# Layer 3 of a four-layer residual network: four of nine depthwise taps moved from TensorE to VectorE, instance-norm scaling moved to ScalarE

**Chip, cores, metric.** One Trainium2 chip, one of its cores. The time is device time in microseconds (us) from the first to the last instruction; lower is better. Unless a spread is given, times are medians of four executions of one kernel in one session (seven for the kernel before, where it was run beside others). The record calls a run slow when it is over 1.5% above the fastest of its kernel; the profiled execution of the kernel before had a mean granted TensorE clock of 0.969 of full speed.

## What is computed

Input x is 4 images of 256 channels and 48 x 48 pixels, f32. Four residual layers follow each other, each on a group norm of x. Layers 0 to 2 are attention, a gate and a second attention, take 4000 us of the 4355 and are not touched. The change is in layer 3:

```python
# x = x + layer3(_gn(x)); in layer3, with x the normalised input:
p = jnp.mean(x, axis=(2, 3))
h = jax.nn.leaky_relu(p @ attn_w1.T, 0.01)
a = jax.nn.sigmoid(h @ attn_w2.T)
y = x * a[:, :, None, None]
y = conv_general_dilated(y, refine_w, padding='SAME', feature_group_count=C)  # 3x3 depthwise
y = y + refine_b[None, :, None, None]
mu = jnp.mean(y, axis=(2, 3), keepdims=True)
var = jnp.mean(jnp.square(y - mu), axis=(2, 3), keepdims=True)
y = (y - mu) * jax.lax.rsqrt(var + 1e-5)
return jax.nn.leaky_relu(y, 0.01)
```

## The kernel before

Channels are split into two halves (k = 0, 1) of 128 partitions; an image half is a tile of 128 x 2304 in SBUF, the on-chip memory. The depthwise convolution runs on TensorE: each tap is a product with a diagonal 128 x 128 matrix, on shifted windows of a padded tile, summed in PSUM, the memory that holds TensorE's sums until another engine reads ("evicts") them. What prepares image b + 1 is a generator (`fill`) that is advanced between the chunks of image b, so that its small steps lie among the work of image b.

```python
def rsqrt(o, i):                              # L157, on GpSimd
    nc.gpsimd.tensor_tensor(o, i, mhalf[:, : i.shape[1]], ALU.pow)

def before_conv(b):                           # prepares image b
    for k in range(NK):
        for s in range(NSL):
            ps = w_mul(b, k, s)               # a matmul that finishes layer 2 (L663)
            nc.scalar.activation(tmp, ps[:, :SL], AF.Identity, bias=..., scale=...)
            nc.gpsimd.tensor_add(X[b][:, k, cols], X[b][:, k, cols], tmp)
            yield
    yield from gn(b, norm)   # 12 bn_stats, aggregate gn_mv, matmul L174, gn_gm, gn_dev,
                             # gn_sq, matmul L184, gn_gv, gn_rs (GpSimd), gn_nb
    ...                      # pm, small matmul, hl, small matmul, sigmoid
    nc.vector.tensor_mul(rsa, norm["rs"], ga)
    nc.vector.tensor_mul(nba, norm["nb"], ga)
    for k in range(NK):
        nc.scalar.activation(pad_of(b, k)[:, 1 : 1 + HW, 1 : 1 + HW], X[b][:, k, :]...,
            AF.Identity, bias=nba[:, k : k + 1], scale=rsa[:, k : k + 1])
    yield

def conv(b, k):
    for c in range(NSL // 2):                 # three chunks of 768 pixels
        ps = sc_tile()
        for h in range(2):
            for t in range(9):
                nc.tensor.matmul(ps[:, h, :SL]..., lhsT=diag[:, k, t, :],
                    rhs=pad[:, r0 + dr : r0 + dr + RS, dc : dc + HW],
                    start=t == 0, stop=t == 8)
        nc.scalar.activation(z[:, cols]..., ps[:, :, :SL], AF.Identity, bias=...)
        for h in range(2):
            nc.vector.bn_stats(st[:, 2 * c + h, :], z[...])
        yield
    nc.vector.bn_aggr(mv, st...)
    nc.vector.tensor_scalar(ve, mv[:, 1:2], IN_EPS, None, ALU.add)
    rsqrt(ri, ve)
    nc.vector.tensor_scalar(z, z, mv[:, 0:1], ri, ALU.subtract, ALU.mult)
    nc.vector.scalar_tensor_tensor(z, z, SLOPE, z, ALU.mult, ALU.max)
    nc.gpsimd.tensor_add(X[b][:, k, :], X[b][:, k, :], z)
    nc.sync.dma_start(ov[:, k, b, :], X[b][:, k, :])
```

## Time and profile before

| | before |
|---|---|
| time, 3 executions before the prediction | 4355.51 us (4351.93 to 4355.94) |
| layer 3: first tap to the end | 4005.5 to 4354.3 us |
| from the first tap of an image to that of the next | 86.2, 86.1, 85.8 us |
| last image, first tap to the end | 90.6 us |
| TensorE records of taps | 864, 293 us |

The names of lines differ between kernels, because the lines move: taps on TensorE L870 before, L873 after; eviction into z L877 and L880; scaling L891 (VectorE) and L902 (ScalarE); leaky step L892 and L903; the last addition on GpSimd L893 and L904; its short additions L819 and L822; padding L851 and L854. The taps on VectorE are L888, new.

### The profile page before, as it was taken

What the parts mean: (1) busy time and instruction counts of PE and PEld (TensorE: products, weight loads), DVE (VectorE), ACT (ScalarE), POOL (GpSimd) and SP (SyncE); (2) the same over time, 40 slices, a digit from 0 to 9 for tenths busy, and PEclk for the clock granted to TensorE, in tenths of its full rate; (3) what the DMA queues carried; (4) which work ended last, traced back from release to release, by engine and by line L of the source; (5) the groups of instructions that cost most, each with busy time, mean ns of one, the idle gap of its engine ahead of it and who ended that gap; (6) DMA issues with size and microseconds to landing.
All of it is one profiled execution on the core that took longest, in us unless ns stands there. A gap on an engine that the chain in (4) does not pass through costs nothing.

```text
span 4354.3 us, 50890 instructions
## 1 busy us (share of the span) xinstructions
PE 4078.9 (94%) x19922; PEld 1805.3 (41%) x19922; DVE 2952.5 (68%) x3719; ACT 1857.8 (43%) x3054; POOL 1065.0 (24%) x632
## 2 busy tenths in 40 slices
PE   7999999999989999999899999998899978899997
PEld 4444444444433344444333444443334433444554
DVE  4555556556989865579898655798975699754222
ACT  3444444444444444444444444444444323343211
POOL 1222222222222322222323222223232221223231
PEclk9999999999999999999999999999999988997999
DMA  4000000000000000000000000000000000000000
GB/s 146 15 15 19 12 15 8 19 15 15 12 11 12 15 12 19 12 15 12 11 15 12 12 19 15 12 15 8 8 1 1 1 1 1 1 1 1 22 33 34
DMA packets 44330, 67.50 MB, mean 16 GB/s; under 512 B 4336, under 2 KB 42032, under 8 KB 42032
## 3 DMA queue, kind: packets, MB, share of 16 engines
q1 hardware_dynamic: 41216, 62.92, 4.7%
q8 instruction: 158, 2.59, 0.3%
q10 hardware_dynamic: 2864, 1.24, 0.1%
q14 instruction: 92, 0.75, 0.1%
HBM read 54.71 MB, written 9.44 MB: 15 GB/s over the span
## 4 chain that ended last, share of the span: by engine, by line
PE 68%; DVE 27%; issue 2%; ACT 2%; POOL 1%; DMA 0%; DVEq 0%; ACTq 0%; POOLq 0%
PE sc L223 24%; PE av L242 23%; DVE acc L262 7%; DVE l1acc L564 7%; PE sc L870 7%; PE pj L397 5%; PE pj L441 3%; PE pj L409 2%; DVE acc L255 2%; DVE rinv L272 2%; PE pj L267 1%; PE pj L663 1%; ACT pt L229 1%; DVE xs L374 1%; PE pj L641 1%
## 5 line engine op out<-in xcount | busy, mean ns | idle before, releaser
L229 ACT ACTIVATE pt<-sc 128x768 f32<-128x768 f32 x1944 | 1473.7, 808 | 1524.1 <-PE sc L223 1429.3
L259 POOL TENSOR_TENSOR half<-pt 128x768 f32<-128x768 f32 x432 | 852.7, 1974 | 2630.6 <-ACT pt L229 2317.2
L223 PE MATMUL sc<-q,k 64*128 64x384 f32 x6912 | 1364.9, 513 | 52.2 <-ACT pt L229 49.4
L242 PE MATMUL av<-pt,v 128*64 128x384 f32 x6912 | 1322.7, 503 | 0.0
L262 DVE TENSOR_TENSOR acc<-acc,pt 128x768 f32<-128x768 f32 x864 | 947.8, 1097 | 128.0 <-ACT pt L229 42.2
L223 PEld LDWEIGHTS sc<-q,k 64*128 64x128 f32 x6912 | 596.5, 187 | 811.3 <-ACT pt L229 304.9
L242 PEld LDWEIGHTS av<-pt,v 128*64 128x64 f32 x6912 | 433.5, 137 | 726.2 <-issue 714.4
L255 DVE TENSOR_TENSOR acc<-acc,half 128x768 f32<-128x768 f32 x432 | 416.4, 964 | 192.0 <-POOL half L259 191.2
L564 DVE SCALAR_TENSOR_TENSOR l1acc<-pd,grid,l1acc 128x256 f32<-128x256 f32 x640 | 347.2, 542 | 18.2
L272 DVE RECIPROCAL rinv<-pj 128x384 f32<-128x384 f32 x108 | 275.9, 2555 | 110.7 <-PE pj L267 110.6
L397 PE MATMUL pj<-xs,w 128*128 128x384 f32 x768 | 303.1, 520 | 40.2 <-issue 32.7
L870 PE MATMUL sc<-pad,diag 128*128 128x384 f32 x864 | 293.0, 499 | 4.5 <-ACT pad L851 4.5
L402 ACT ACTIVATE pj<-pj 128x384 f32<-128x384 f32 x192 | 91.2, 475 | 402.6 <-DVE q L401 266.1
L870 PEld LDWEIGHTS sc<-pad,diag 128*128 128x128 f32 x864 | 165.8, 194 | 130.0 <-issue 16.0
L397 PEld LDWEIGHTS pj<-xs,w 128*128 128x128 f32 x768 | 136.2, 193 | 186.0 <-issue 101.5
L441 PE MATMUL pj<-o,wo 128*128 128x384 f32 x384 | 175.8, 540 | 39.2 <-DVE x L450 16.5
L450 DVE TENSOR_TENSOR x<-pj,x 128x384 f32<-128x384 f32 x144 | 79.9, 555 | 170.1 <-PE pj L441 170.1
L223 PE MATMUL sc<-qv,kd 64*128 64x384 f32 x864 | 176.6, 527 | 19.1 <-ACT pt L229 19.1
L242 PE MATMUL av<-pt,qv 128*64 128x384 f32 x864 | 192.1, 534 | 0.0
L409 PE MATMUL pj<-w,xs 128*128 128x128 f32 x1152 | 152.8, 283 | 13.7 <-DVE x L450 12.2
L409 PEld LDWEIGHTS pj<-w,xs 128*128 128x128 f32 x1152 | 139.2, 193 | 60.2 <-issue 28.9
L252 DVE TENSOR_TENSOR acc<-pt 128x768 f32<-128x768 f32 x108 | 107.1, 992 | 45.4 <-ACT pt L229 45.1
(137 smaller groups left out, 2102.4 us busy)
## 6 DMA issues: line engine op xcount, KB each, us to landing
xs<-in_x_dram SPq DMA_DIRECT2D x96, 384.0 KB, 3.3
x<-in_x_dram SPq DMA_DIRECT2D x8, 1152.0 KB, 8.6
out_dram<-x SPq DMA_DIRECT2D x8, 1152.0 KB, 4.2
w<-in_wqkv_dram SPq DMA_DIRECT2D x32, 192.0 KB, 3.7
wo<-in_wout_dram ACTq DMA_DIRECT2D x1, 512.0 KB, 4.8
dw<-in_dww_dram ACTq DMA_DIRECT2D x1, 132.0 KB, 5.4
wph<-in_thphi_w_dram ACTq DMA_DIRECT2D x2, 64.0 KB, 4.6
Ww<-in_W_w_dram ACTq DMA_DIRECT2D x2, 64.0 KB, 5.3
```

What stands on the lines that cost most here:

```text
L223: nc.tensor.matmul(ps[:, h, :SL], lhsT=u["of"]["k"][r, j * P : (j + 1) * P], rhs=u["of"]["q"][r, u["qc"]], start=True, stop=True,)
L229: nc.scalar.activation(pt, ps[:, :, :SL], AF.Exp)
L242: nc.tensor.matmul(u["av"][r, :SL], lhsT=value(u, j, h), rhs=pt[:, h, :], start=j == 0, stop=j == JB - 1,)
L255: nc.vector.tensor_add(u["acc"], u["acc"], u["half"])
L259: nc.gpsimd.tensor_add(u["half"], pts[0], pts[1])
L262: nc.vector.tensor_add(u["acc"], u["acc"], pt)
L272: nc.vector.reciprocal(u["rinv"], u["l"][:, :SL])
L397: nc.tensor.matmul(ps[:, :SL], lhsT=w[:, k, t, :], rhs=xs[s][:, k, :], start=k == 0, stop=k == NK - 1,)
L409: nc.tensor.matmul(ps[:, i * P : (i + 1) * P], lhsT=xs[s][:, k, i * P : (i + 1) * P], rhs=w[:, k, 2, :], start=k == 0, stop=k == NK - 1,)
L441: nc.tensor.matmul(ps[:, :SL], lhsT=wo[:, p, k * P : (k + 1) * P], rhs=o, start=True, stop=True)
L564: nc.vector.scalar_tensor_tensor(acc, src, w, acc, ALU.mult, ALU.add)
L870: nc.tensor.matmul(ps[:, h, :SL].rearrange("p (r c) -> p r c", c=HW), lhsT=diag[:, k, t, :], rhs=pad[:, r0 + dr : r0 + dr + RS, dc : dc + HW],
```

## The change

The intent: TensorE is full in layer 3, so four taps of nine go to VectorE as a fused multiply-add over the whole half, and one pass over z goes from VectorE to ScalarE to make room. The statistics move behind the taps, since they need the finished sum.

```diff
-    diag = lp.tile([P, NK, 9, P], F32, name="diag")
+    PE_TAPS = (0, 1, 2, 3, 5)
+    DVE_TAPS = (4, 6, 7, 8)
+    diag = lp.tile([P, NK, len(PE_TAPS), P], F32, name="diag")
 ...                                   (building the diagonals: the same, for PE_TAPS only)
-                for t in range(9):
+                for t in PE_TAPS:
 ...
-            for h in range(2):
-                s = 2 * c + h
-                nc.vector.bn_stats(st[:, s, :], z[:, s * SL : (s + 1) * SL])
             yield
+        zr = z.rearrange("p (r c) -> p r c", c=HW)
+        for t in DVE_TAPS:
+            dr, dc = divmod(t, 3)
+            nc.vector.scalar_tensor_tensor(
+                zr, pad[:, dr : dr + HW, dc : dc + HW], rfw[:, k, t : t + 1], zr,
+                ALU.mult, ALU.add,
+            )
+        for s in range(NSL):
+            nc.vector.bn_stats(st[:, s, :], z[:, s * SL : (s + 1) * SL])
 ...
-        nc.vector.tensor_scalar(z, z, mv[:, 0:1], ri, ALU.subtract, ALU.mult)
+        nc.vector.scalar_tensor_tensor(mr, mv[:, 0:1], -1.0, ri, ALU.mult, ALU.mult)
+        nc.scalar.activation(z, z, AF.Identity, bias=mr, scale=ri)
```

More of the change, by code (lines that the diff above doesn't have):

```diff
@@ L789, in usual_path @@
     nc.vector.tensor_add(bi2, bi2, vec[:, V_B2, :])
-    diag = lp.tile([P, NK, 9, P], F32, name="diag")
+    PE_TAPS = (0, 1, 2, 3, 5)
+    DVE_TAPS = (4, 6, 7, 8)
+    diag = lp.tile([P, NK, len(PE_TAPS), P], F32, name="diag")
     for k in range(NK):
-        for t in range(9):
-            nc.gpsimd.tensor_scalar(diag[:, k, t, :], ident, rfw[:, k, t : t + 1], None, ALU.mult)
+        for i, t in enumerate(PE_TAPS):
+            nc.gpsimd.tensor_scalar(diag[:, k, i, :], ident, rfw[:, k, t : t + 1], None, ALU.mult)
     W2 = HW + 2
@@ L867, in conv @@
                 r0 = (2 * c + h) * RS
-                for t in range(9):
+                for t in PE_TAPS:
                     dr, dc = divmod(t, 3)
@@ L871, in conv @@
                         ps[:, h, :SL].rearrange("p (r c) -> p r c", c=HW),
-                        lhsT=diag[:, k, t, :],
+                        lhsT=diag[:, k, PE_TAPS.index(t), :],
                         rhs=pad[:, r0 + dr : r0 + dr + RS, dc : dc + HW],
-                        start=t == 0, stop=t == 8,
+                        start=t == PE_TAPS[0], stop=t == PE_TAPS[-1],
                     )
@@ L890, in conv @@
         rsqrt(ri, ve)
-        nc.vector.tensor_scalar(z, z, mv[:, 0:1], ri, ALU.subtract, ALU.mult)
+        mr = small.tile([P, 1], F32, tag="in_mr", name="in_mr")
+        nc.vector.scalar_tensor_tensor(mr, mv[:, 0:1], -1.0, ri, ALU.mult, ALU.mult)
+        nc.scalar.activation(z, z, AF.Identity, bias=mr, scale=ri)
         nc.vector.scalar_tensor_tensor(z, z, SLOPE, z, ALU.mult, ALU.max)
```

## The prediction

- A "lock" is here no more than a name for what the traces show: a VectorE and a GpSimd instruction that run together, and one or both last longer by up to the time of the other. The kernel before shows it for pairs of additions like the one quoted (3.44 us for 2.02 and 2.59 for 1.80). That a tap and an addition do the same, and that the one that starts later waits until the other ends, was an estimate in the prediction; the changed kernel then showed it (a tap of 6.40 us for 2.62, begun 1.06 us after an addition of 5.03 us and done 2.43 us after it).
- 2.62 us for a tap: in the kernel before, passes of VectorE with two operands take 958 ns for 768 columns (L262) and 2558 for the 2304 of L892. On the line through both, 256 columns take 425 ns; the layer 1 taps take 485, 0.06 us more, and 2.56 + 0.06 is 2.62. This is an estimate from those three medians.
- "Cold", and the 1.7 us charged for it: in the kernel before the granted clock was 0.87, 0.89 and 0.79 in the first chunk of the first three images and 1.00 in the second. That a stall of 3 us would bring such a dip too, the one us taken off the sum, is my estimate and was not shown.

> **What bounds the kernel now.** I read the page first, then the last stage alone. The change touches only layer 3, so the first question is where layer 3 lies and what sets its length. The groups by line, for the last 455 us:
>
> ```profile
> L870 PE MATMUL sc<-pad,diag 128*128 128x384 f32 x864 | 293.0, 499 | 4.5 <-ACT pad L851 4.5
> ...
> L893 POOL TENSOR_TENSOR x<-x,z 128x2304 f32<-128x2304 f32 x8 | 40.4, 5051 | 26.6 <-DVE z L892 26.6
> ...
> L892 DVE SCALAR_TENSOR_TENSOR z<-z 128x2304 f32<-128x2304 f32 x8 | 21.4, 2674 | 0.1
> ...
> L891 DVE TENSOR_SCALAR z<-z,in_mv,in_ri 128x2304 f32<-128x2304 f32 x8 | 13.8, 1728 | 5.7 <-POOL in_ri L157 5.7
> ```
>
> The reader is to see that the nine diagonal taps (L870, two records for each f32 matmul) are busy for 293 us, start at 4005.5 us and wait for almost nothing, while the other engines have little. The waits say the same from the other side:
>
> ```profile
> ACT z L877 <- PE sc L870: 257.7, 24, 12.3
> ```
>
> The chain that ended last shows two things besides: what lies between the convolution of one image and that of the next, and what follows the last one. First the border between image 0 and 1, then the end:
>
> ```profile
> 4072.99 11.72 PE sc L870 x36
> ...
> 4084.86 0.17 DVE gn_gv L186
> ...
> 4085.10 0.71 POOL gn_rs L157
> ...
> 4086.12 0.41 PE pj L828 x4
> ...
> 4089.37 2.21 ACT pad L851
> ...
> 4091.72 8.48 PE sc L870 x21
> ```
>
> ```profile
> 4263.66 72.47 PE sc L870 x216
> 4336.15 0.91 ACT z L877
> 4337.08 1.03 DVE in_st L883 x2
> 4339.37 1.49 DVE z L891
> 4340.89 2.57 DVE z L892
> 4343.62 5.00 POOL x L893
> ```
>
> So TensorE binds except for a border of 7 us per image (convolution ends at 4084.7, the next begins at 4091.7) and a tail of 12.5 us plus 5.7 us of the last store. One chunk (768 pixels, 18 matmuls, 36 records) takes 11.65 us, an image 86.1 us from first matmul to first matmul (4005.5, 4091.7, 4177.9, 4263.7).
>
> [...] In the timeline of layer 1, the same pair of adds takes 2.02 us alone and 3.44 us beside a GpSimd add, which itself grows to 2.59 us from its usual 1.80:
>
> ```profile
> 1172.18 3.44 DVE L262 TENSOR_TENSOR acc<-acc,pt 128x768 f32<-128x768 f32 x2
> 1180.40 2.02 DVE L262 TENSOR_TENSOR acc<-acc,pt 128x768 f32<-128x768 f32 x2
> 1172.22 2.59 POOL L259 TENSOR_TENSOR half<-pt 128x768 f32<-128x768 f32 x1 [9.60 <-DVE acc L255]
> ```
>
> [...] L892, a two-input operation of that size, has a median of 2558. [...] the pad writes (L851) take 2305 ns. [...] the first chunk after each border took 13.3 to 14.6 us against 11.65, so I charge about 1.7 us.
>
> **Removed from TensorE.** 4 of 9 taps: 384 of 864 records. A chunk becomes 20/36 of 11.65 = 6.45 us, an image saves 6 x 5.2 = 31.2 us, all four 125 us (2.9%). This would be the gain if nothing else changed.
>
> **Added to VectorE.** 32 taps over 2304 elements, both inputs in SBUF, each waiting for the one before (in place). L892 is the same operation with an immediate, 2.55 us. The layer 1 taps have a pointer scalar and a strided window like the new ones:
>
> ```profile
> L564 DVE SCALAR_TENSOR_TENSOR l1acc<-pd,grid,l1acc x640: 461/485/2131, 1145.2 to 3710.2; 128x256 f32<-128x256 f32 x160
> ```
>
> [...] a tap is 2.62 us, 2.65 with the gap: 85 us in all. L891 leaves VectorE (13.8 us) and becomes ScalarE work of about 2.3 us each. By sums VectorE has per image some 8 x 2.65 + 12 x 0.5 (stats) + 12 x 0.5 (group-norm stats) + 2 x 2.6 + 2 = 40 us, and TensorE 39 + 9 (the twelve L663 products at 0.74) = 48 us. TensorE would still be the longer, so the question is the order. GpSimd builds 10 diagonals instead of 18 (5 us less), but its next operation on the path (L157, at 3977.4) waits for VectorE; no gain.
>
> **The order.** The listing of both programs shows that VectorE now runs the group norm of image b+1 in between the taps of image b: statistics 9 to 12 between the four taps of half 0, and gn_nb, hl, hl, rsa/nba each behind one tap of half 1. The pad of the next image, which TensorE needs, thus waits for all four taps of half 1, whose input is the last chunk. On GpSimd gn_rs stands behind the 5.05 us addition of half 0's result. I walk through one image, t = 0 at its first matmul:
>
> - TensorE: chunk 0 to 8.1 (cold), chunks 1 and 2 and five products to 24.7; ScalarE evacuates, z of half 0 is whole at 25.7.
> - Four taps of half 0. After each a statistic waits for a GpSimd addition (0.99 us), which the tap just locked out, and the next tap is then locked out by the next addition: about 3.65 us a tap. They end at 40.3. Six statistics (0.47 each) to 43.6, the group-norm aggregate at 43.9.
> - TensorE: chunks 0 and 1 of half 1 and four products end near 41.1; then the small matmul L174 wants that aggregate: a stall of about 3 us, new. Rest of chunk 2 until E = 50.2.
> - ScalarE scaling 45.8 to 48.1, leaky step (L892's successor) to 50.7. GpSimd starts its 5.05 us addition at 50.85, just before tap 1 of half 1 gets its input (51.2): tap 1 is locked out until 55.9 and ends at 58.5. Then gn_rs to 59.2, gn_nb, pm; tap 2 to 62.2; hl; tap 3 to 65.05; hl, sigmoid; tap 4 to 67.9; rsa, nba; pad 68.3 to 70.5. Next image at 70.6.
>
> The border grows from 7 to about 20 us and an image shrinks only from 86.1 to 70.6: 15.5 us saved of 31.2, three times, 46.5.
>
> **The last image** has no filling. Chunks end at 40.5. Half 0: taps 22 to 32.7, scaling, leaky step to 42. Half 1: tap 1 to 44.6, GpSimd's addition of half 0 takes the lock to 49.7, taps 2 to 4 to 57.6, statistics 60.5, aggregate and reciprocal root 62.1, ScalarE 64.4, leaky 67, addition 72.2, store 78. Before: 90.6 us. Saved 12.5: of 31.2, some 18.7 go to the longer tail.
>
> **Sum.** 46.5 + 12.5 = 59; one us off for a dip of the clock after the new stall: 58. Time 4355.5 - 58 = 4298 us, -1.3%.
>
> **Rivals.**
> 1. Full gain: VectorE's 40 us hide beside 48 us of TensorE, only a border of about 9 us and the tail of four taps (10.5 us) remain: about 4250 us. For it: the sums, and 150.6 us that VectorE waits for ScalarE now. Against: the order puts the pad behind the taps.
> 2. The same order, but the lock costs little (GpSimd fits between, or TensorE's stall at L174 vanishes): a border of 15 us, 3 x 23 + 18 = 87 saved, 4268 us. For it: only an overlap of a few tenths decides who gets the lock. Against: even unlocked, gn_rs stays behind the 5 us addition on its queue.
> 3. VectorE becomes the bound: taps of 4 us and more by locks, image 80 us: 4325 us. For it: layer 1 taps reach 2131 ns. Against: GpSimd has only about 22 us of additions per image.
> 4. Slower: would need over 31 us lost per image. I see nothing that large.
>
> **Range and chances.** My walk uses measured durations; its uncertain part is who wins the lock, some 2 to 5 us per image, and the clock after longer borders, 1 to 2. That makes 15 us each way common. Range 4275 to 4325. Over 2% faster (below 4268) needs rival 1 or the lucky end of 2: 0.09. Slower by 2%: 0.01.
>
> **What would show it.** Right: 480 records of taps; about 6.45 us a chunk; image starts 70 us apart; L174 waiting some 3 us for the aggregate; pads waiting for nba behind tap 4, border 18 to 21 us; mean tap above 3 us, minimum near 2.6; last matmul to end about 37 us instead of 18. Wrong: image starts 63 us or less apart (rivals 1, 2), a mean tap near 2.6, the pad ready before the last taps, or a border below 15 us.

## More of the kernel before

The view that the prediction leaves out is the load of each engine in one stretch. Its columns are: the stretch in us, its length, then the busy time (and the number of instructions) of TensorE, TensorE's weight loads, VectorE, ScalarE and GpSimd, the granted clock, the DMA share and GB/s. First the three images from first tap to first tap, in the kernel before:

```profile
4005.49:4263.66 258.17, 249.07 (x750) 139.22 (x751) 69.61 (x133) 52.30 (x63) 69.68 (x49) 0.96 0.06 23
```

TensorE works 249 of 258 us, VectorE 70. That is the invitation for the change: one engine is full, three are three quarters empty.

## The result, and the profile after

The changed kernel takes 4289.84 us (4288.64 to 4290.33), the kernel before 4354.71 us in the same session (4351.93 to 4355.94). The ratio is 0.9852, with a 95% interval of 0.9834 to 0.9869: 1.5% faster, inside the predicted range of 4275 to 4325 us. (Ratios here are the mean time of one kernel's fast runs over that of the other's fast runs of the same rounds, so not quite the ratio of the medians quoted.)

| | before | predicted | after |
|---|---|---|---|
| time | 4355.5 | 4298 | 4289.8 us |
| first tap of layer 3 | 4005.5 | | 4002.4 us |
| image periods | 86.2, 86.1, 85.8 | 70.6 | 69.2, 68.7, 69.7 us |
| last image | 90.6 | 78 | 77.9 us |
| border: L184, which follows the last tap, to the next image's first tap | 7.2 | 20 | 19.3 us |

In the two profiled executions the saving is 66.5 us: 50.7 in three periods, 12.7 in the last image and 3.1 before layer 3. Up to there the programs differ only in the diagonals that GpSimd builds (10 for 18, 5.8 us for 10.5), and TensorE was already 3.1 us ahead when that began (its L663 products just before start at 3955.6 us for 3958.7). I do not count these 3.1 as an effect: executions of the kernel before differ by 4 us among themselves.

The same view of load as above, for the three periods of the changed kernel:

```profile
4002.35:4209.87 207.52, 159.38 (x463) 86.69 (x463) 130.71 (x154) 63.62 (x68) 93.73 (x48) 0.86 0.07 29
```

No engine is full now: TensorE works 159 of 208 us, VectorE 131. TensorE saved 90 us of work, and only 51 of them came through. So the end must be set by an order of waits. (The granted clock fell from 0.96 to 0.86 in these views, but that is not where the time went: the first chunk of the first three images took 1.4 to 3.0 us longer than the second in the changed kernel, 8.15 to 9.67 for 6.72 us, at a granted clock of 0.65 to 0.83 for 1.00, and 1.4 to 2.8 us before, 13.32 to 14.63 for 11.88, at 0.79 to 0.89 for 1.00.) The groups by line of the changed kernel over its last 390 us (busy us, mean ns of one, then the idle time of the engine before them):

```profile
L873 PE MATMUL sc<-pad,diag 128*128 128x384 f32 x480 | 169.1, 510 | 5.7 <-ACT pad L854 5.7
L888 DVE SCALAR_TENSOR_TENSOR z<-pad,rfw,z 128x2304 f32<-128x2304 f32 x32 | 102.1, 3190 | 30.8 <-ACT z L880 30.6
...
L822 POOL TENSOR_TENSOR x<-x,tmp 128x384 f32<-128x384 f32 x48 | 69.8, 1471 | 74.6 <-ACT tmp L818 74.6
...
L904 POOL TENSOR_TENSOR x<-x,z 128x2304 f32<-128x2304 f32 x8 | 42.7, 5332 | 31.6 <-DVE z L903 31.6
```

The taps on TensorE are 480 records and 169 us, as counted. A tap on VectorE takes 3.19 us in the mean, though the view of that one line gives its shortest, median and longest as 2610, 2619 and 7271 ns: most are short, a few wait inside. The border between image 0 and 1 in the timeline (start, duration, engine, line, what it does, idle time before it) shows where:

```profile
4052.32 5.03 POOL L904 TENSOR_TENSOR x<-x,z 128x2304 f32<-128x2304 f32 x1 [5.27 <-DVE z L903]
...
4053.38 6.40 DVE L888 SCALAR_TENSOR_TENSOR z<-pad,rfw,z 128x2304 f32<-128x2304 f32 x1 [0.66 <-ACT z L880]
4057.31 3.02 POOL L157 TENSOR_TENSOR gn_rs<-gn_gv,mhalf 128x2 f32<-128x2 f32 x1
...
4060.51 2.61 DVE L888 SCALAR_TENSOR_TENSOR z<-pad,rfw,z 128x2304 f32<-128x2304 f32 x1
...
4065.81 2.62 DVE L888 SCALAR_TENSOR_TENSOR z<-pad,rfw,z 128x2304 f32<-128x2304 f32 x1
...
4068.42 0.15 DVE L852 TENSOR_TENSOR nba<-gn_nb,ga 128x2 f32<-128x2 f32 x1
...
4069.06 4.51 ACT L854 ACTIVATE pad<-x,nba,rsa 128x2304 f32<-128x2304 f32 x2
...
4071.51 3.96 PE L873 MATMUL sc<-pad,diag 128*128 128x384 f32 x7 [0.56 <-ACT pad L854]
```

The taps of image 0 on TensorE ended at 4052.2. The first VectorE tap of half 1 starts while GpSimd's addition runs, and is not done until 2.4 us after it. gn_rs, an operation on two columns, starts after the addition and finishes only 0.55 us after that tap. Then every small step of image 1 waits for one tap; nba is last, and TensorE starts image 1 at 4071.5. The end of the chain that ended last has the same pair in the last image, a tap of 7.28 us:

```profile
4252.60 2.54 DVE z L888
4255.16 7.28 DVE z L888
4262.46 2.63 DVE z L888
4265.12 2.63 DVE z L888
4267.77 2.87 DVE in_st L893 x6
...
4277.13 5.03 POOL x L904
```

### The profile page after: what moved, and what is told of

Its sections match the earlier page's. It is cut to its first block, busy times and chain, and to the rows that moved or that the text cites. A ratio compares the mean times of both kernels' runs of the same rounds, so it can differ in the third digit from the quotient of the medians.

```text
span 4287.8 us, 50150 instructions
## 1 busy us (share of the span) xinstructions
PE 3954.9 (92%) x19538; PEld 1733.6 (40%) x19538; DVE 3034.9 (71%) x3751; ACT 1875.7 (44%) x3062; POOL 1088.3 (25%) x624
## 4 chain that ended last, share of the span: by engine, by line
PE 64%; DVE 29%; issue 3%; ACT 2%; POOL 2%; DMA 0%; DVEq 0%; ACTq 0%; POOLq 0%
PE sc L223 24%; PE av L242 23%; DVE acc L262 8%; DVE l1acc L564 7%; PE pj L397 5%; PE pj L441 3%; PE pj L409 2%; DVE acc L255 2%; PE sc L873 2%; DVE rinv L272 2%; DVE z L888 2%; PE pj L267 1%; PE pj L663 1%; ACT pt L229 1%; DVE xs L374 1%
## 5 line engine op out<-in xcount | busy, mean ns | idle before, releaser
L259 POOL TENSOR_TENSOR half<-pt 128x768 f32<-128x768 f32 x432 | 853.8, 1976 | 2626.5 <-ACT pt L229 2313.1
L262 DVE TENSOR_TENSOR acc<-acc,pt 128x768 f32<-128x768 f32 x864 | 946.1, 1095 | 128.1 <-ACT pt L229 42.3
L873 PE MATMUL sc<-pad,diag 128*128 128x384 f32 x480 | 169.1, 510 | 5.7 <-ACT pad L854 5.7
L252 DVE TENSOR_TENSOR acc<-pt 128x768 f32<-128x768 f32 x108 | 107.1, 992 | 45.2 <-ACT pt L229 44.8
L166 DVE BATCH_NORM_STATS2 gn_st<-x 128x6 f32<-128x384 f32 x192 | 98.1, 549 | 57.4 <-POOL x L822 57.4
```

What stands on the lines that cost most here:

```text
L259: nc.gpsimd.tensor_add(u["half"], pts[0], pts[1])
L262: nc.vector.tensor_add(u["acc"], u["acc"], pt)
L873: nc.tensor.matmul(ps[:, h, :SL].rearrange("p (r c) -> p r c", c=HW), lhsT=diag[:, k, PE_TAPS.index(t), :], rhs=pad[:, r0 + dr : r0 + dr + ...
```

## The experiments

Theory: TensorE's saving is genuine (125 us), but about half of it is lost, because (a) the four long taps of a half stand in VectorE's queue before small operations that the next image needs, (b) GpSimd's operations and VectorE's taps lock each other out, (c) in the last image the taps stand behind TensorE. Rivals: VectorE is simply full; or the scaling on ScalarE is what helped or hurt. Twelve kernels were run, in four sessions, each on another chip by the record. In these the kernel before took 4352.2 to 4353.9 us; the changed kernel was not run again, its 4289.84 us belong to the session in which the kernel before took 4354.7. So the medians may be compared to about 3 us. In four expectations a phrase is cut at the mark: three gave the rival a reason that no run here shows; the fourth, of the scaling alone, named a rate of the pass that was not measured (that rival was: taking the scaling off VectorE relieves the border by itself).

### No taps on VectorE at all

```diff
-        for t in DVE_TAPS:
-            ... nc.vector.scalar_tensor_tensor(zr, pad[...], rfw[:, k, t : t + 1], zr, ...)
```

Wrong on purpose: the output lacks four taps (relative error 0.25).

> The changed kernel with the four VectorE taps simply left out (wrong result on purpose): what TensorE's saving is worth when nothing is put on VectorE. My theory (125 us less of taps on TensorE, of which the taps on VectorE give back about 60 at the image borders and in the tail): about 4232 us, image starts 55 us apart. Rival (the taps hide, and the lost gain is due to something else, such as the clock after shorter bursts or the scaling on ScalarE): close to the changed kernel, 4280 us or more.

Measured 4228.09 us (4225.18 to 4232.65), ratio 0.9714, at a mean granted clock of 0.970 for 0.963 with the taps. The saving of TensorE's part is 125 us, as counted from the records, and VectorE's taps cost 61.7 us of it, though they are busy for only 102 us of the 285 that layer 3 lasts with them. By the profiles the loss is 44.8 us in the three periods (162.7 us without these taps, 207.5 with them) and 17.4 us in the last image (60.6 and 77.9). Of the 44.8, 39.5 are the three borders together (17.7 and 57.2 us) and 4.7 three new stalls at L174.

### The scaling alone

```diff
+    PE_TAPS = tuple(range(9))
+    DVE_TAPS = ()
 ...                          (bn_stats again inside the chunk loop, as in the kernel before)
```

> Nine taps on TensorE and statistics per chunk as before, only the scaling on ScalarE. My theory: it is off the path but for the last image, where 2.3 us on ScalarE and one small operation stand for 1.5 us on VectorE: 4355 to 4358 us, same within 0.1%. Rival [...]: 4345 us or less.

Measured 4354.61 us (4353.95 to 4357.13), ratio 1.0005 with an interval of 0.9989 to 1.0022. The scaling on ScalarE (2.30 us a pass for 1.73 on VectorE) is worth nothing by itself; gain and loss come with the taps. What the scaling is worth beside taps on VectorE was not tested.

### The long taps of half 1 behind the next image's small steps

```diff
+        last["nba", b] = nc.vector.tensor_mul(nba, norm["nb"], ga)
 ...
+            tap = nc.vector.scalar_tensor_tensor(
 ...
+            if k == 1 and t == DVE_TAPS[0] and b + 1 < B:
+                after_(tap, last["nba", b + 1])     # order on VectorE, no semaphore
```

> The changed kernel with one order edge per image: tap 1 of half 1 comes behind the last group-norm operation of the next image (nba) on VectorE. Theory (the pad waits because four taps stand before it): the border shrinks from 19.4 to about 12 us, as gn_rs still waits for the 5 us addition on GpSimd; 3 times 7 us: about 4269 us. Rival (VectorE's amount of work is the bound, not its order): no gain, 4285 to 4295.

Measured 4268.89 us (4268.17 to 4271.94), ratio 0.9808. Periods of 61.0, 62.1 and 62.5 us for 69.2, 68.7 and 69.7: part (a) of the theory is worth 21 us. What is left of the border in this kernel (11.1 us) is mainly one wait (TensorE is idle for 5.8 us before the next small product), in its timeline:

```profile
4052.97 5.03 POOL L915 TENSOR_TENSOR x<-x,z 128x2304 f32<-128x2304 f32 x1 [5.27 <-DVE z L914]
...
4057.96 0.70 POOL L157 TENSOR_TENSOR gn_rs<-gn_gv,mhalf 128x2 f32<-128x2 f32 x1
4058.69 0.16 DVE L190 SCALAR_TENSOR_TENSOR gn_nb<-gn_gm,gn_rs 128x2 f32<-128x2 f32 x1 [5.34 <-POOL gn_rs L157]
```

gn_rs (now at its usual 0.70 us, as no tap runs) stands in GpSimd's queue behind the 5 us addition. The next experiment takes it out of there.

### In addition, GpSimd's addition behind gn_rs

```diff
+        add = nc.gpsimd.tensor_add(X[b][:, k, :], X[b][:, k, :], z)
+        if k == 0 and b + 1 < B:
+            held.append((add, b + 1))               # later: after_(add, gn_rs of b + 1)
```

> As e3_hold, and the addition of half 0 on GpSimd comes behind gn_rs of the next image. Theory: the border falls to the 7 us of before; 3 times 12 us against the changed kernel: about 4254 us. Rival (the addition on GpSimd costs nothing): same as e3_hold.

Measured 4268.62 us (4267.08 to 4271.73), no change: the expectation failed by 15 us. The order did change as meant, and the timeline of this kernel shows what took its place:

```profile
4055.63 0.69 POOL L157 TENSOR_TENSOR gn_rs<-gn_gv,mhalf 128x2 f32<-128x2 f32 x1 [5.74 <-DVE gn_gv L186]
4056.29 5.03 POOL L918 TENSOR_TENSOR x<-x,z 128x2304 f32<-128x2304 f32 x1
4056.36 4.98 DVE L190 SCALAR_TENSOR_TENSOR gn_nb<-gn_gm,gn_rs 128x2 f32<-128x2 f32 x1 [0.81 <-POOL gn_rs L157]
```

gn_rs is done early, GpSimd goes straight on to its addition, and gn_nb, a VectorE operation on two columns with both operands in SBUF, comes 0.07 us later and lasts 4.98 us in place of 0.16. One 5 us wait was exchanged for another.

### GpSimd's last addition replaced by fills

```diff
-        nc.gpsimd.tensor_add(X[b][:, k, :], X[b][:, k, :], z)
-        nc.sync.dma_start(ov[:, k, b, :], X[b][:, k, :])
+        nc.gpsimd.memset(z, 0.0)
+        last["fill", b, k] = nc.gpsimd.memset(z, 0.0)
+        nc.sync.dma_start(ov[:, k, b, :], z)
 ...                                   (and gn_rs of b + 1 kept behind the fills of half 0)
```

> Wrong on purpose: GpSimd's last addition x + z (two operands read from SBUF, 5.03 to 5.3 us) is replaced by two fills of z with zeros, which only write SBUF and take about as long together; the transfer out sends z, and the small gn_rs keeps its place behind the fills. Order and volume of everything else stay. Theory (the long VectorE taps are held up by GpSimd's addition, and not merely late): the tap that took 6.40 us at the border and the one that took 7.28 us in the last image fall to 2.6 us each, gn_rs falls from 3.02 to 0.7 us. At each of the three borders some 2.3 to 3 us go, in the last image some 4.6 us: about 4276 us in all, between 4273 and 4280. Rival (those taps are long for another reason, for example they wait for the activation's write or for the profiler's modelled ends): nothing moves, 4286 to 4290.

Measured 4274.62 us (4274.3 to 4276.17), ratio 0.9818. Its output is wrong (relative error 1.0). The kernel is otherwise the changed one, taps in their old place. The view of the taps' line (shortest, median, longest in ns) and the border's first steps:

```profile
L899 DVE SCALAR_TENSOR_TENSOR z<-pad,rfw,z x32: 2611/2619/2882, 4029.2 to 4250.2; 128x2304 f32<-128x2304 f32 x32
```

```profile
4052.22 2.02 POOL L915 MEMSET z<- 128x2304 f32 x1 [5.19 <-DVE z L914]
...
4053.35 2.62 DVE L899 SCALAR_TENSOR_TENSOR z<-pad,rfw,z 128x2304 f32<-128x2304 f32 x1 [0.66 <-ACT z L891]
4054.30 2.02 POOL L916 MEMSET z<- 128x2304 f32 x1
4056.28 0.69 POOL L157 TENSOR_TENSOR gn_rs<-gn_gv,mhalf 128x2 f32<-128x2 f32 x1
```

No tap is longer than 2.88 us, gn_rs is back at 0.69, and the tap runs undisturbed beside the fills, which only write. So the 6.4 and 7.3 us were made by GpSimd's reading addition. The kernel is 15.2 us faster than the change; the two fills took 4.06 us for the addition's 5.03, and gn_rs stands behind them, so about 1 us at each of three borders, and 1 us after the last leaky step, is the shorter work. Part (b), for this one operation, is worth 11 to 15 us.

### The taps by chunk

```diff
+            for t in DVE_TAPS:                      # inside the chunk loop, on 768 pixels
+                nc.vector.scalar_tensor_tensor(zr, pad[:, 2*c*RS + dr : 2*(c+1)*RS + dr, ...], ...)
+            for h in range(2):
+                nc.vector.bn_stats(...)
             yield
```

> The four taps and bn_stats work on one chunk of 768 pixels right after its eviction, in place of one pass over the 2304 pixels of a half after its three chunks. VectorE then does 96 taps of 768 elements for 32 of 2304; by the 2.62 us of the long form and the fixed part that the short ones show, a tap takes about 1.02 us, so VectorE works some 14 us longer in all. Theory (what is left of the change is lost because a half's taps come in one block behind its last chunk, where gn_st, gn_nb and the last statistics have to queue behind them): the wait at L174 of 2.9 us and the long border go, border about 12 us for 19.4, and the last image ends some 13 us sooner since only one chunk's taps stand behind TensorE's last chunk. Sum 3 times 8 to 9 and 13: about 4250 us, between 4245 and 4260. Rival (VectorE's work is the bound, its place does not matter): slower than the change by up to the 14 us, 4288 to 4304.

Measured 4270.75 us (4268.25 to 4272.68), ratio 0.981: 19 us faster than the change, but 21 short of the expectation. The length of a short tap, which I had estimated from 2.62 us for 2304 columns and 485 ns for 256, came out as expected too: 1.019 us in the median. So did the last image (67.6 us for 77.9): part (c) is real. The borders did not: 17.9 us (from the end of the last tap, since L184 itself waits here). The small steps now find VectorE's queue full of short taps, in the timeline of this kernel:

```profile
4041.73 7.80 DVE L887 SCALAR_TENSOR_TENSOR z<-pad,rfw,z 128x768 f32<-128x768 f32 x3
...
4049.45 0.15 DVE L176 COPY gn_gm<-pj 128x2 f32<-128x2 f32 x1
...
4053.28 0.15 DVE L178 TENSOR_TENSOR gn_dev<-gn_mv,gn_gm 128x2 f32<-128x2 f32 x1
...
4055.38 0.15 DVE L181 TENSOR_TENSOR gn_sq<-gn_sq,gn_mv 128x2 f32<-128x2 f32 x1
...
4055.59 0.59 PE L184 MATMUL pj<-gn_sq,gmat 128*128 128x2 f32 x2 [7.15 <-DVE gn_sq L181]
```

Three short taps took 7.80 us in all, because GpSimd's addition of half 0 came between (the longest single one was 5.71 us); gn_gm waits for them, and each further step for one or two taps more. TensorE waits 7.15 us at L184. My expectation had only counted the steps after gn_rs. Shorter instructions do not help where the order stays wrong.

### Both at the border: long taps and GpSimd's addition behind nba

```diff
+            if k == 1 and t == DVE_TAPS[0] and b + 1 < B:
+                held.append((tap, b + 1, NoSync))
 ...
+        if k == 0 and b + 1 < B:
+            held.append((add, b + 1, Sync))         # GpSimd waits for nba of b + 1
```

> As e4_hold_pool, where the first long tap of the second half is kept behind the next image's nba on VectorE; but GpSimd's addition of the first half now waits, by a semaphore, until nba is done, not only behind gn_rs. In e4 it started 0.07 us before gn_nb and held this operation of two columns for 4.98 us. Theory (the lock ate e4's gain): gn_nb takes 0.16 us again, the border goes from 11.1 us in e3 to about 7 us, three times about 4 us less the extra delay in the last steps: about 4256 us, between 4253 and 4260. Rival (the border is set by the chain of small operations itself, whatever GpSimd does): 4266 to 4270 as e3 and e4.

Measured 4270.79 us (4267.13 to 4271.99), no faster than with the long taps held alone. Yet the border is down to 6.0 us (TensorE: 4052.8 to 4058.8), and the first period is 55.9 us. The following periods are 63.0 and 64.2 us, the last image 82.1. The timeline of image 1:

```profile
4056.19 13.23 DVE L896 SCALAR_TENSOR_TENSOR z<-pad,rfw,z 128x2304 f32<-128x2304 f32 x3
...
4056.42 7.31 POOL L914 TENSOR_TENSOR x<-x,z 128x2304 f32<-128x2304 f32 x1 [2.36 <-DVE nba L860]
...
4063.68 10.82 POOL L830 TENSOR_TENSOR x<-x,tmp 128x384 f32<-128x384 f32 x4
...
4081.63 2.72 PE L663 MATMUL pj<-y,Ww 64*128 64x384 f32 x4 [2.72 <-ACT tmp L826]
```

The lock moved, it did not go. Released together, taps and addition now meet inside image 1; GpSimd's four short additions behind them take 10.8 us (1.0 each when alone), their tmp buffers come free late, ScalarE's evictions and TensorE's products (L663) wait: from 4078.9 to 4084.3 TensorE has no tap to do and is idle half of the time. The gain at the border was given back 20 us later.

### The same with the taps by chunk

```diff
-            if k == 1 and t == DVE_TAPS[0] and b + 1 < B:                (in e8)
+                if k == 1 and c == NSL // 2 - 1 and t == DVE_TAPS[0] and b + 1 < B:
```

> e6_chunk and e8_hold_all together: taps by chunk, and at a border the taps of the last chunk and GpSimd's addition of the first half stand behind the next image's nba. If the gains at the borders add to the shorter tail: border about 7 us for e6's about 12, so three times 4 to 5 us below e6, about 4237 us, between 4232 and 4243. Rival (by chunk the border's wait is no longer behind taps, so holding them back gains nothing): the same as e6 within 3 us.

Measured 4268.66 us (4265.18 to 4271.48), within 3 us of the taps by chunk alone; the expectation failed by 32 us, and the rival's number came true, though not its reason: the border did get short (9.5 us from the end of the last tap, first period 57.8 us), but the next two periods are 65.2 and 66.1: inside the image TensorE has no tap to do from 4077.2 to 4084.5 and is idle for 4.7 us of it, as before.

### The last addition on VectorE

```diff
-        add = nc.gpsimd.tensor_add(X[b][:, k, :], X[b][:, k, :], z)
+        add = nc.vector.tensor_add(X[b][:, k, :], X[b][:, k, :], z)      (rest as e8)
```

In the kernel before, an f32 addition of 768 columns takes 958 ns on VectorE (L262) and 1813 on GpSimd (L259), and a pass with two operands over 2304 columns takes 2558 ns on VectorE (L892); here the addition of 2304 columns takes 5.03 us on GpSimd. So an estimate for VectorE is 2.6 us, against 5 us for which the addition and a tap hold each other up. The trace of this run agrees: 2.55 and 2.56 us in the last image, 2.68 in the mean of the five before.

> As e8_hold_all (long taps of the second half behind the next image's nba), but the last addition x + z goes to VectorE for both halves, that of the first half also behind nba. GpSimd then keeps only the short additions of 384 columns. Theory (in e8 the border shrank to 5.9 us, but the gain went to the next image, where GpSimd's long addition took 7.31 us beside a tap, the short ones behind it came late and TensorE waited 2.7 us and more for the tmp of ScalarE): with the 5.03 us addition gone from GpSimd the waits inside the image go, and VectorE pays about 2.6 us for each of 8 additions, which fit into its idle time of some 15 us per image. Period from conv to conv about 58 to 60 us for e8's 62.9, the last image about 74 us for e8's 82: about 4254 us, between 4246 and 4262. Rival (VectorE, at about 46 us of work per image, [...] are the bound, so moving work there costs what it saves): 4266 to 4275.

Measured 4252.82 us (4251.77 to 4254.09), ratio 0.9768 (0.9752 to 0.9785). Periods 55.9, 59.5 and 57.9 us, last image 74.5. Two groups of the profile from 4000 to 4190 us:

```profile
L896 DVE SCALAR_TENSOR_TENSOR z<-pad,rfw,z 128x2304 f32<-128x2304 f32 x24 | 66.1, 2754 | 4.4 <-ACT z L888 4.2
L914 DVE TENSOR_TENSOR x<-x,z 128x2304 f32<-128x2304 f32 x5 | 13.4, 2676 | 0.0
```

More work on the engine that got the taps made the kernel 18 us faster than the version with the long addition on GpSimd. A tap takes 2.75 us in the mean; in that version, over layer 3, it was 3.45. VectorE is busy for 121 of the 173 us of the three periods. The rival (VectorE is the bound) falls at this split.

### And the last image by chunk

```diff
+            if b == B - 1:
+                taps(k, pad, z, st, c, c + 1)
             yield
+        if b < B - 1:
+            tap = taps(k, pad, z, st, 0, NSL // 2)
```

> As e10_vector_add, with the taps of the last image alone done by chunk of 768 pixels, as in e6_chunk, where the last image took 67.6 us for the 77.9 us of the change. The small steps of an image's border are not touched, since the last image has none after it. Theory (the tail is set by one half's four long taps behind TensorE's last chunk): 7 to 10 us below e10_vector_add. Rival (the tail of e10 is bound by VectorE's total work in the last image, which grows by some 5 us through 24 short taps for 8 long ones): equal to e10 within 2 us or slower.

Measured 4246.88 us (4245.71 to 4250.86), ratio 0.9755 (0.9739 to 0.9772): 5.9 us less than the last one, a little under the expected 7 to 10. The last image went from 74.5 to 70.3 us. Why not to the 67.6 of the first kernel by chunk: here the taps of the previous image's second half, held behind nba, and what follows them (statistics, leaky step, addition) lie on VectorE inside the last image, up to 4205.2 us, and the additions of the last image itself are on VectorE too. From 4185.7 us to the end of the last addition at 4240.2 VectorE is busy for 50 of 54.5 us. How much each of the two costs was not tested. This is the best version found: 43 us below the change, and correct.

### Other splits of the nine taps, in the best version

```diff
-    PE_TAPS = (0, 1, 2, 3, 5)            # split 5 + 4
-    DVE_TAPS = (4, 6, 7, 8)
+    PE_TAPS = (0, 1, 2, 3)               # split 4 + 5; the other run: (0 ... 5) and (6, 7, 8)
+    DVE_TAPS = (4, 5, 6, 7, 8)
```

> e12_last_by_chunk with four taps on TensorE and five on VectorE. TensorE saves one tap of nine: two records of 0.32 us for each 384 columns, 1.3 us per chunk, 7.8 us per image; VectorE pays two more long taps per image, 5.2 us, on top of about 46 us. In e10 the period from conv to conv is 57.8 us, of which TensorE is nearly always busy. Theory (TensorE is still the bound there, VectorE has room): up to 7.8 us per image less, but the waits for the short GpSimd additions behind long taps grow, so I expect half of it: about 4 us an image, 4231 us, between 4222 and 4240. Rival ([...] VectorE is full at five taps): 4246 to 4260, no faster.

> e12_last_by_chunk with six taps on TensorE and three on VectorE: the opposite step. Theory (TensorE is the bound in layer 3 once the borders are short): 7.8 us per image more, four images, 31 us, less perhaps 4 us for waits behind taps that go: about 4274 us, between 4268 and 4280. Rival (VectorE [...] are the bound): faster than e12_last_by_chunk, 4230 to 4245.

Measured 4257.07 us (4254.58 to 4258.22) with four taps on TensorE, ratio 0.978, and 4258.33 us (4255.67 to 4260.06) with six, ratio 0.9782. Both are slower than five and four (4246.88 us): the intervals of the ratios overlap, but the slowest of its runs, 4250.9 us, is below the fastest of theirs, 4254.6. Both expectations were off; with four taps on TensorE the time lies in the range of the rival, with six in neither. With five taps VectorE comes late at two places, in the waits of that kernel over layer 3 (us in all, times, longest):

```profile
ACT z L902 <- DVE x L923: 21.8, 3, 8.2
...
PE pj L174 <- DVE gn_mv L171: 11.0, 3, 5.7
...
PE sc L895 <- ACT z L902: 9.5, 3, 5.8
```

ScalarE can't evict a chunk into z, because VectorE's addition (L923) has not yet read the z of two halves before; PSUM stays occupied and TensorE waits: 9.5 us, which the best version does not have, besides 11.0 at L174 (5.4 there). The three periods are 3.1 us longer in sum than in the best version, the last image 6.1 us (76.4 for 70.3). VectorE is busy for 78 and 88% of the second and third period and 86% of the last image: there the rival holds in good part. With six taps TensorE's wait at L174 is gone altogether and it pays only 4 us an image for the extra tap in place of 7.8 (the periods are 61.7 for 57.5 us in the mean): over the last two of them its busy time grew by 6.7 us per image and its idle time shrank by 3.0. So at five and four TensorE isn't a pure bound either; of the three splits tried it is the best.

## Why the prediction was right, point by point

- **TensorE saves 125 us.** Right: 480 records, and the kernel without VectorE taps is 125 us below the kernel before (4228.1 for 4353.4 in its session). (20/36 of 11.65 us is 6.47, not the 6.45 of the working, which changes nothing.)
- **A tap is 2.62 us.** Right: the median is 2.619. (The leaky step in the same kernel, a fused operation with an immediate and no shifted window, takes 2.559; the runs don't tell whether the scalar or the window makes the difference of 0.06 us.)
- **The scaling on ScalarE does nothing of note.** The prediction only gave its cost, 2.3 us; measured 2.30, and alone it changes the time by 0.05%, which the interval does not tell from zero.
- **Half 0's taps about 3.65 us each from 25.7 us of the image, ending at 40.3; the group-norm aggregate at 43.9; then a stall of 3 us at L174.** The end at 40.3 is right by luck: z of half 0 was whole at 26.8 us, 1.1 later than in the working, and the taps followed each other every 3.35 us in the mean, not 3.65, so two errors cancel. The aggregate was done at 43.7 (at 43.9 it is that of the instance norm, just behind it). TensorE too came 1.1 us later to L174 (42.2 for 41.1), so the stall was 1.55 us, half of what was predicted, in each of the three images. (A wait of 2.93 us at L174 lies before the first image, in both kernels; the expectation of the taps by chunk took it for this one.) The mechanism is as predicted: GpSimd's four short additions, 1.00 us each alone, and the taps hold each other up, in the timeline of image 0:

```profile
4029.22 2.62 DVE L888 SCALAR_TENSOR_TENSOR z<-pad,rfw,z 128x2304 f32<-128x2304 f32 x1 [4.23 <-ACT z L880]
...
4029.93 10.26 POOL L822 TENSOR_TENSOR x<-x,tmp 128x384 f32<-128x384 f32 x4 [5.54 <-ACT tmp L818]
...
4039.73 2.88 DVE L888 SCALAR_TENSOR_TENSOR z<-pad,rfw,z 128x2304 f32<-128x2304 f32 x1
...
4046.11 0.38 PE L174 MATMUL pj<-gn_mv,gmat 128*128 128x2 f32 x2 [1.55 <-DVE gn_mv L171]
```

- **The border of 20 us, by the lock and by the small steps behind taps.** Measured 19.3 by the same steps in the same order. That both causes are real is shown apart: order alone 21 us (long taps held back), long addition alone 11 to 15 us (fills). Both act on the same borders, so they may not be added; held taps with the long addition moved to VectorE are 37 us faster than the change.
- **The last image 78 us.** Measured 77.9; the locked tap was 7.28 us.
- **The sum was 58, the profiles show 66.5.** Of the 8.5 us between them 3.1 lie before layer 3 and are not the change's. About 4.3 are three image periods of 69.2 in place of 70.6: the term that was mis-sized is the way from half 0's aggregates to its scaling, for which the prediction took 1.9 us (43.9 to 45.8) and which took 1.2 (43.7 to 44.9). What follows came about 1 us sooner (GpSimd's addition at 50.0 for 50.85, the end of tap 1 at 57.4 for 58.5); the other 0.4 us came from the steps behind tap 1. The last image gave 12.7 for 12.5. The last 1 us was the allowance for a clock dip after the new stall, and the trace shows none: the 18 records of taps behind the stall take 6.05 us, 18 in half 0's last chunk, behind no stall, 6.07; the granted clock in the stretch behind it (4046.1 to 4052.2 us) was 1.00.
- **Rival 1, full gain at 4250**, had the right sums but not for this order: the work does hide, 4246.9 us, once the small steps come first, the long addition leaves GpSimd and the last taps are cut. **Rival 2, the lock costs little, 4268**, is denied by the fills: the lock of the long addition costs 11 to 15 us. Without it the border is 15.9 us, near the 15 of this rival. **Rival 3, VectorE as the bound**, is false at four taps and holds in good part at five.

What stays open: the part of the loss that GpSimd's 48 short additions cost by their share of the lock (1.47 us in the mean for 1.00 alone) was not measured apart. And the 3.1 us before layer 3 were not pursued.

## What to carry to other kernels

Summed busy time told nearly nothing here: VectorE was under two thirds busy (131 of 208 us), and half of TensorE's saving was still lost, in good part because long instructions had been put in front of two-column operations on which the next image waits. Before moving work to another engine, write down that engine's order of instructions around the place where the full engine next needs something, and look there for pairs: a VectorE tap beside GpSimd's addition, which reads x and z, took 6.40 us for 2.62, but 2.62 beside a GpSimd fill of 2.02 us, which only writes. Operations on two columns suffered as much as large ones: gn_nb took 4.98 us for 0.16 beside that addition, GpSimd's gn_rs 3.02 for 0.70 beside a tap. In the trace the time is in the duration of the instruction held up, not in the idle time before it (0.66 us before the tap of 6.40). Where such a pair meets, moving the slower one to VectorE can be cheaper than leaving it on GpSimd: with the addition of 2304 columns moved, the kernel here took 4252.8 us for 4270.8. A wait that is taken away at one border has to be looked for inside the next stage, as three of these experiments show.
